# A two-layer convolution and attention kernel: first products fed from the weight sums in SBUF, a first image normalised by two engines, and earlier transposes

## The chip, the cores and the metric

The kernel runs on one NeuronCore of one Trainium2 chip. The metric is the device time of one execution in microseconds (us). Three runs of the kernel before took 2762.28, 2762.81 and 2766.79 us; the median is 2762.81 us. A separate execution was recorded by the hardware profiler; every duration, wait and instant below is from that one.

In the text, PE is the tensor engine (matmul), DVE the vector engine, ACT the scalar engine, POOL the GpSimd engine and SP the engine whose queue issues nearly all DMAs.

## What is computed

Eight images of 768 channels and 32x32 pixels (1024 tokens) pass through two residual layers. Cut to what matters:

```python
# layer 0: attention on a group-normalised image
qkv = gn(x) as tokens @ W_qkv.T            # only k and v are used
scores = var(v) @ var(k).T * scale         # one variance per token and head: rank one
out = softmax(scores) @ v                  # 12 heads of 64
x = x + (out @ W_proj.T + b_proj)
# layer 1: local correlations and a 1x1 convolution
f = gn(x)
corr = 28 shifted products of f / |f| with itself, summed over channels
x = x + (conv_w @ concat(f, corr) + conv_b)
```

All data and weights are float32.

## The kernel before

**The products.** Every large product (keys and values, the projection, the convolution) is split into 2x2 blocks, and the 8 block products are replaced by 7 products of sums of blocks (the scheme of Strassen and Winograd). A product has a number p; the numbers in use order are `ORDER = (1, 5, 6, 3, 7, 4, 2)`. Products 1, 3 and 2 of keys and values take blocks of the weights as they are; 5, 6, 7 and 4 take sums of weight blocks. One unit of `KeysValues.unit` is one such product for one pair of token tiles g: six matmul records of 128x384, because each of three contraction chunks takes two passes. A half (384 columns of the weights) has two rounds d of 14 units in the order of `PAIR`, which alternates two token pairs. The operands on the image's side also need sums, `s`, which POOL makes in `make_sums`: first the sum of two blocks for both pairs (L546), then three more sums from it (L548, L550, L552).

**The weight sums.** `WeightSums(which, ...)` loads four blocks of weights into one buffer (`ws`), and its four steps make the sums on DVE and store each into DRAM (`kvs` for the two halves of keys and values, `tsp` and `tsc` for projection and convolution). `KvStream` then streams the weight blocks of all units through five buffers (`KVBLOCKS`), from the weights themselves or from `kvs`. The buffer of `ws` is the single buffer of the pool `fpool`, which also holds the images `f` and `raw1`; so the sums of the second half can be loaded only when those of the first are done with.

**The first image.** The prologue loads image 0 (`xn`, six chunks of 128x1024) and the weights of sum 0 over the queues of SP and ACT. `first_norm` takes its statistics on DVE, spreads them over groups with two small matmuls, raises to the power -1/2 on POOL (`rstd`), and `Norm.apply` normalises the six chunks on DVE. Between the third and the fourth chunk the first weight sum is made; the other three follow the sixth chunk. All four are stored by DMAs on ACT's queue and loaded back by `KvStream`.

**The order.** Nothing is scheduled by hand on the chip: while the program is written out, an object `Clock` keeps a model time, and work is appended to the engines' queues when its model time has come (`later.after(us, job)`; `later.after_dve(us, job)` counts from the end of the vector work that the model knows). Each engine then runs its queue strictly in order and waits where a semaphore asks for it. So the figures in these calls decide only the order of instructions on each queue.

**One image in steady state** takes about 338 us. Its second half of keys and values, its attention (six pairs of heads; `av` matmuls in bursts of 16 or 32 records), the correlations and the convolution of the image before, its own projection, and the first half of the next image follow each other on PE. `KeysValues.spread` closes each half: DVE computes the variances (`vm`, `km`) and their maximum, POOL spreads the maximum, and then the function `values` transposes the variances of v on PE (`ptv`, L501), DVE copies them (`rsv`), a DMA writes them to DRAM (`vdr`) and DMAs broadcast them to all partitions (`bc`), from which ACT makes exponentials (`ex`, L674), which are what the `av` matmuls stream. `keys` does the same for k (`nk`, `ptk`, `rsk`, `kdr`, `bk`), from which ACT sums denominators (`junk`, L684). For each of the first three pairs of heads, the sums are inverted (`inv`), transposed on PE (`it`), copied (`ir`), written (`di`), broadcast (`rd`), and multiplied into the output (`v<-v,rd` on DVE). There are six buffers of `ex` and two of each of the matmul banks x and y; z products use the y banks.

Of the kernel before, what the change touches and what calls it, by code (L numbers as in the profile page):

```python
# [6 lines left out]
F32 = mybir.dt.float32  # L7
AF = mybir.ActivationFunctionType
ALU = mybir.AluOpType
# [4 lines left out]
P = 128  # L14
NB, C, H, W = 8, 768, 32, 32
# [23 lines left out]
JH = J // 2  # L39
# [23 lines left out]
ORDER = (1, 5, 6, 3, 7, 4, 2)  # L63
# [88 lines left out]
def two_layers(ctx, tc, x, wkv, wproj, bproj, wconv, wcorr, bconv, out):  # L152
    nc = tc.nc

    def pool(name, bufs, **kw):
        return ctx.enter_context(tc.tile_pool(name=name, bufs=bufs, **kw))
# [17 lines left out]
    st = pool("st", 1)  # L174
# [8 lines left out]
    later = clock  # L183
    vector = Vector(nc.vector, clock)
    ready = set()
# [14 lines left out]
    def image_tile(pl, tag, name):  # L200
        return pl.tile([P, J, N], F32, tag=tag, name=name)
# [24 lines left out]
    class WeightSums:  # L226


        def __init__(self, which, *queues):
            self.which = which  # L230
            flat = image_tile(fpool, "f", f"ws{which}").rearrange("p j n -> p (j n)")
            self.at = [flat[:, n * JH * KW : (n + 1) * JH * KW] for n in range(5)]
            for n in range(4):
                r, c = divmod(n, 2)
                queue = queues[n % len(queues)]
                if which in (0, 1):
                    queue.dma_start(out=self.at[n].rearrange("p (k m) -> p k m", k=JH), in_=kv_block(which, r, c))
                else:
                    to = self.at[n].rearrange("p (k m) -> p k m", k=JH)
                    queue.dma_start(out=to, in_=t_block(which, r, c).rearrange("p k i m -> p k (i m)"))  # L240
# [14 lines left out]

        def step(self, engine, p, to, a, b, op, queue):
            engine.tensor_tensor(to, a, b, op)
            self.store(p, to, queue)

        def store(self, p, at, queue):  # L260
# [5 lines left out]

    class KvStream:
        def __init__(self):
            self.keys = [(b, h, d, p) for b in range(NB) for h in range(2) for d in range(2) for p in ORDER]
            self.loaded, self.tiles, self.gone = 0, {}, set()  # L270

        def fill(self, most=None):
# [9 lines left out]

        def done(self, key):
            del self.tiles[key]

            def free():
                self.gone.add(key)
                self.fill()

            later.after(KV_US + 0.3, free)  # L290
# [64 lines left out]
    xn = load(image_tile(xnpool, "xn", "xn0"), xv[0], nc.sync, nc.scalar)  # L355
    sums0 = WeightSums(0, nc.sync, nc.scalar)
    kv_stream, t_stream = KvStream(), TStream()
# [68 lines left out]
    class Norm:  # L426
# [24 lines left out]
            self.rstd = st.tile([P, 1], F32, tag="rstd", bufs=2, name=f"rstd{name}")  # L451
            nc.gpsimd.tensor_tensor(self.rstd, ve, neghalf[:, 0:1], ALU.pow)  # L452

        def apply(self, to, src, key, apart, between=lambda: None):


            def chunk(j):
                vector.tensor_scalar(to[:, j, :], src[:, j, :], self.mean, self.rstd, ALU.subtract, ALU.mult)
                if j + 1 == JH:
                    between()  # L460
                if j + 1 < J:
                    later.after(apart, lambda: chunk(j + 1))
                else:
                    ready.add(key)

            chunk(0)

    def first_norm(b, xn, apart, then):

        bn = gn_tile(f"bn1_{b}")  # L470

        def stats(j):
            for hf in range(2):
                gn_stats(bn, xn, j, hf)
            if j + 1 < J:
                later.after(2 * apart, lambda: stats(j + 1))
            else:
                norm = Norm(bn, f"a{b}")
                later.after_dve(0.3, norm.means)
                later.after_dve(3.0, norm.spreads)  # L480
                later.after_dve(5.0, lambda: then(norm))

        stats(0)
# [22 lines left out]
    class KeysValues:  # L506
# [101 lines left out]
        def spread(self, half):  # L608
            b = self.b
            name = f"{b}_{half}"  # L610
            km2 = st.tile([P, HH, MT], F32, tag="km2", bufs=2, name=f"km2{name}")
            head_m2(self.bn["k", half], km2, f"k{name}")
            top = st.tile([P, HH], F32, tag="top", name=f"top{name}")
            vector.tensor_reduce(top, km2, AX.X, ALU.max)
            most = st.tile([P, HH], F32, tag="most", name=f"most{name}")
            nc.gpsimd.partition_all_reduce(most, top, P, bass_isa.ReduceOp.max)
            m2 = st.tile([P, HH, MT], F32, tag="vm2", bufs=4, name=f"vm2{name}")
            head_m2(self.bn["v", half], m2, f"v{name}")
            nk = st.tile([P, HH, MT], F32, tag="nk", bufs=4, name=f"nk{name}")
            kdr, vdr = [dpool.tile([HH, N], F32, tag=f"{kind}dr", name=f"{kind}dr{name}") for kind in "kv"]  # L620
            for of, new in ((self.m2, m2), (self.nk, nk), (self.kdr, kdr), (self.vdr, vdr)):
                of.append(new)

            def values():
                to_rows(m2, vdr, f"v{name}")
                ready.add(("v", b, half))

            def keys():
                for h in range(HH):
                    vector.tensor_scalar(  # L630
                        nk[:, h, :], km2[:, h, :], most[:, h : h + 1], HD ** -0.5 / (HD - 1) ** 2,
                        ALU.subtract, ALU.mult,
                    )
                ready.add(("nk", b, half))
                if not set(SUMMED[b > 0]).issuperset(range(3 * half, 3 * half + 3)):
                    later.after_dve(0.5, rows)

            def rows():
                to_rows(nk, kdr, f"k{name}")
                ready.add(("k", b, half))  # L640

            later.after_dve(2.5, values)
            later.after_dve(3.5, keys)


    class Pair:
# [538 lines left out]
    def project(b, ots):  # L1185
        f = first_f[0] if b == 0 else image_tile(fpool, "f", f"f{b}")
        for n, us in ((0, 0.0), (1, 0.5), (3, 1.5), (4, 3.0), (2, 12.0), (5, 14.0)) if b else ():
            later.after(us, lambda n=n: nc.sync.dma_start(out=f[:, n, :], in_=xv[b, :, n, :]))
        bn = gn_tile(f"bn2_{b}")
        if b + 1 < NB:  # L1190
            x1_dram[b] = dpool.tile([P, J, N], F32, tag="x1", name=f"x1d{b}")
        left = {(i, hf) for i in range(J) for hf in range(2)}

        def finished(i, hf):
            gn_stats(bn, f, i, hf)
            left.remove((i, hf))
            if b + 1 < NB and (i, 1 - hf) not in left:
                nc.sync.dma_start(out=x1_dram[b][:, i, :], in_=f[:, i, :])
            if not left:
                later.after(0.1, normalise)  # L1200

        def normalise():
            norm = Norm(bn, f"b{b}")
            later.after_dve(0.3, norm.means)
            later.after_dve(3.0, norm.spreads)

            def apply():
                to = f if b + 1 < NB else image_tile(xnpool, "xn", "f_last")
                layer1.append((to, f))
                norm.apply(to, f, ("f", b), 2.0 if b + 1 < NB else 0.0)  # L1210

            later.after_dve(5.0, apply)

        sums = TokenSums(f"o{b}", ots[:JH], ots[JH:])
        clock.wait(("ot", b, JH - 1), ready=ready)
        sums.first()
        wide = Wide("p", f"p{b}", f, bproj_sb, sums.operand, finished)
        late = True
        for n, (us, _, unit) in enumerate(wide.units()):
            if n == 4:  # L1220
                clock.wait(("ot", b, HP - 1), ready=ready)
            if late and n > 1 and ("ot", b, HP - 1) in ready:
                late = False
                sums.second()
                later.after(3.0, sums.thirds)
                later.after(8.0, sums.fourth)
            unit()
            clock.pass_time(us)
# [6 lines left out]
        xn = images[b]  # L1235
        clock.after(12.0, lambda: first_norm(b, xn, 1.2, lambda norm: norm.apply(xn, xn, ("xn", b), 1.2)))

    steps0 = sums0.steps(vector, nc.scalar)
    kv_stream.fill(1)

    def first_sum():
        steps0[0]()
        kv_stream.fill(2)

    first_norm(0, xn, 0.0, lambda norm: norm.apply(xn, xn, ("xn", 0), 0.0, first_sum))
    clock.wait(("xn", 0), ready=ready)
    for step in steps0[1:]:
        step()
    kv_stream.fill()
    images, layer1 = [xn], []  # L1250
    first_f = []

    def sum_weights(which, wait):
        for n, step in enumerate(WeightSums(which, nc.sync).steps(vector, nc.sync)):
            later.after(wait + 3.0 * n, step)

    def load_first_f():
        first_f.append(load(image_tile(fpool, "f", "f0"), xv[0]))
# [17 lines left out]
            later.after(1.0 * n, t_stream.fill)  # L1276

    second = []
    sum_weights(1, 24.0)
    later.after(50.0, lambda: sum_weights("p", 14.0))  # L1280
    later.after(82.0, load_second)
    kv, kv1 = KeysValues(0, xn), KeysValues(1, None)
    work_off(kv.units(0))
    for b in range(NB + 1):
# [6 lines left out]
        if b:  # L1291
# [3 lines left out]
            f, acc = layer1[b - 1] if b > 1 else first_f * 2  # L1295
# [66 lines left out]
```

## Time and profile before

| what | value |
|---|---|
| median of 3 runs | 2762.81 us |
| time of the profiled execution | 2773.49 us |
| its span (first to last instruction) | 2771.8 us |
| granted TensorE clock, mean | 0.993 |
| PE busy | 2712.3 us (98%) |
| DVE busy | 1664.1 us (60%) |
| ACT busy | 1362.3 us (49%) |
| POOL busy | 307.0 us (11%) |
| DMA moved | 451.85 MB, 163 GB/s over the span |

The profiled execution took 10.7 us more than the median of the runs. PE is the engine that is nearly always busy, so the time can be read as PE's work plus the moments in which PE waits or runs slowly. These are few: before 40 us, in the first attention, and a few microseconds in each later image. An idle moment of any other engine matters only where PE then waits for it.

In the answers of the trace, a row of a timeline gives the start in us, the duration in us, the engine, the line, the operation, output<-inputs, the shape and the number of instructions merged into the row; brackets at its end give the engine's idle time just before and what ended it. Ends of matmuls are modelled, so a row of matmuls reads some 0.2 us longer than the distance to the next.

### The profile page before, as it was taken

To read this page: it belongs to the slowest core of one execution; us is meant where nothing else is said; L and a number is where in the kernel's file an instruction comes from. 1 tells how busy PE (TensorE), PEld (TensorE's weight loads), DVE (VectorE), ACT (ScalarE), POOL (GpSimd) and SP (SyncE) were. 2 spreads that over 40 slices of the span, in tenths; PEclk is the share of its full clock that TensorE was granted. 3 is DMA by queue.
4 is the path that set the end of the run, shared out by engine and by line. 5 is a ranking of instruction groups with operands and counts; after the bars stand their busy time and mean duration, and the time that the engine had idled before them with its cause. 6 is when DMAs were issued, how large, how long until landed. Compare 5 with 4: busy or idle time off the path is not lost.

```text
span 2771.8 us, 28821 instructions
## 1 busy us (share of the span) xinstructions
PE 2712.3 (98%) x9063; PEld 1277.7 (46%) x9063; DVE 1664.1 (60%) x4163; ACT 1362.3 (49%) x1814; POOL 307.0 (11%) x350
## 2 busy tenths in 40 slices
PE   6999999999999999999999999999999999999999
PEld 3543454335643455434554346533465334653353
DVE  4858734685447854478534884358743587446853
ACT  1398078520596106970079701886019850298400
POOL 3420101002200031000310012100121001110000
PEclk9999999999999999999999999999999999999999
DMA  8764454545554545536456365563654536535323
GB/s 302 280 227 150 142 189 122 163 165 160 175 150 143 187 154 157 165 128 204 150 158 189 97 203 168 149 181 91 228 175 130 182 97 222 171 113 170 117 73 95
DMA packets 324579, 451.85 MB, mean 163 GB/s; under 512 B 59794, under 2 KB 245890, under 8 KB 324426
## 3 DMA queue, kind: packets, MB, share of 16 engines
q1 hardware_dynamic: 322618, 444.88, 50.8%
q10 hardware_dynamic: 1808, 5.11, 0.5%
q8 instruction: 73, 1.20, 0.2%
q14 instruction: 80, 0.66, 0.1%
HBM read 380.44 MB, written 67.38 MB: 162 GB/s over the span
## 4 chain that ended last, share of the span: by engine, by line
PE 74%; issue 10%; DMA 5%; ACT 5%; DVE 4%; SPq 1%; POOL 1%; DVEq 0%; POOLq 0%; ACTq 0%
PE x L342 29%; PE av L699 17%; PE y L342 14%; PE z L342 8%; ACT ex L674 3%; PE gr L1006 2%; DMA rd<-di 2%; ACT junk L684 2%; DMA bc<-vdr 1%; DVE dn L146 1%; PE den L732 1%; PE z L936 1%; PE x L936 1%; PE den L782 1%; DVE cs L146 0%
## 5 line engine op out<-in xcount | busy, mean ns | idle before, releaser
L674 ACT ACTIVATE ex<-bc,nk 128x1024 f32<-128x1024 f32 x768 | 834.5, 1138 | 493.6 <-DMA bc<-vdr 271.3
L699 PE MATMUL av<-ex,v 128*64 128x512 f32 x3072 | 709.1, 601 | 12.3 <-ACT ex L674 12.3
L684 ACT ACTIVATE junk<-bk,vm 128x1024 bf16<-128x1024 f32 x368 | 420.5, 1143 | 41.9 <-DMA bk<-kdr 35.6
L699 PEld LDWEIGHTS av<-ex,v 128*64 128x64 f32 x3072 | 218.7, 138 | 473.9 <-issue 394.4
L146 DVE TENSOR_TENSOR acc<-acc,ex 128x1024 f32<-128x1024 f32 x350 | 401.6, 1212 | 0.0
L209 ACT COPY kp<-x 128x384 f32<-128x384 f32 x28 | 13.3, 479 | 558.1 <-PE x L342 558.1
L342 PE MATMUL y<-kv,s 128*128 128x384 f32 x768 | 267.8, 489 | 2.6 <-DMA kv<-kvs 2.6
L342 PE MATMUL x<-kv,xn 128*128 128x384 f32 x768 | 263.9, 490 | 4.4 <-DVE xn L146 3.3
L342 PE MATMUL x<-kv,s 128*128 128x384 f32 x768 | 262.2, 489 | 3.3 <-POOL s L546 3.3
L342 PEld LDWEIGHTS x<-kv,xn 128*128 128x128 f32 x768 | 145.1, 191 | 108.6 <-issue 14.3
L342 PEld LDWEIGHTS x<-kv,s 128*128 128x128 f32 x768 | 145.4, 191 | 104.1 <-issue 6.8
L342 PEld LDWEIGHTS y<-kv,s 128*128 128x128 f32 x768 | 142.4, 190 | 102.1 <-issue 8.7
L1006 PE MATMUL gr<-f 128*128 128x227 f32 (+1 forms) x672 | 131.8, 346 | 0.0
L342 PE MATMUL z<-kv,xn 128*128 128x384 f32 x384 | 130.1, 488 | 0.0
L342 PE MATMUL x<-v,wt 128*128 128x512 f32 x288 | 130.0, 596 | 0.0
L1006 PEld LDWEIGHTS gr<-f 128*128 128x128 f32 x672 | 121.2, 190 | 18.7 <-issue 6.2
L146 DVE TENSOR_TENSOR v<-y,v 128x128 f32<-128x128 f32 x180 | 40.9, 282 | 136.5 <-PE y L342 136.5
L342 PE MATMUL x<-f,wt 128*128 128x512 f32 x252 | 115.4, 598 | 0.1
L452 POOL TENSOR_TENSOR rstda<-vea,neghalf 128x1 f32<-128x1 f32 x8 | 4.8, 597 | 930.2 <-DVE vea L146 930.2
L546 POOL TENSOR_TENSOR s<-xn 128x384 f32<-128x384 f32 x64 | 68.5, 1080 | 309.6 <-PE x L342 219.4
L146 DVE BATCH_NORM_STATS2 vbn<-v 128x6 f32<-128x64 f32 x720 | 101.7, 210 | 0.0
L146 DVE COPY acc<-ex 128x1024 f32<-128x1024 f32 x50 | 33.7, 703 | 107.6 <-ACT junk L684 36.8
(170 smaller groups left out, 2925.0 us busy)
## 6 DMA issues: line engine op xcount, KB each, us to landing
kv<-kvs SPq DMA_DIRECT2D x128, 576.0 KB
kv<-in_wkv_dram SPq DMA_DIRECT2D x96, 576.0 KB
bc<-vdr SPq DMA_DIRECT2D x96, 512.0 KB
f<-in_x_dram SPq DMA_DIRECT2D x48, 512.0 KB
bk<-kdr SPq DMA_DIRECT2D x46, 512.0 KB
x1d<-f SPq DMA_DIRECT2D x42, 512.0 KB
x<-x1d SPq DMA_DIRECT2D x42, 512.0 KB
out_dram<-x SPq DMA_DIRECT2D x84, 256.0 KB
```

The lines of the kernel that those rows point to most:

```text
L146: return getattr(self.engine, name)(*args, **kw)
L209: nc.scalar.copy(to, at)
L342: nc.tensor.matmul(t, lhsT=lhsT, rhs=rhs, start=p in FIRST and k == 0, stop=stop and k == len(pairs) - 1, skip_group_check=True,)
L452: nc.gpsimd.tensor_tensor(self.rstd, ve, neghalf[:, 0:1], ALU.pow)
L546: nc.gpsimd.tensor_tensor(self.sums[g][:, 0], a[g][2], a[g][3], ALU.add)
L674: nc.scalar.activation(ex, self.bc[e], AF.Exp, scale=self.kv.nk[self.half][:, h, t : t + 1])
L684: nc.scalar.activation(junk, self.bk[e], AF.Exp, scale=self.kv.m2[self.half][:, h, t : t + 1], accum_out=self.sums[:, e, t : t + 1],)
L699: nc.tensor.matmul(self.av[e * HD : (e + 1) * HD, hf, :], lhsT=self.vt[:, t, e, :], rhs=exs[e][:, hf * HF : (hf + 1) * HF], start=t == 0, ...
L732: nc.tensor.matmul(den[at * 32 : (at + 1) * 32, :], lhsT=ones[:, 0:32], rhs=self.acc[e][:, hf * HF : (hf + 1) * HF], start=True, stop=True,)
L782: nc.tensor.matmul(den[e * HD : (e + 1) * HD, :], lhsT=ones, rhs=self.acc[e][:, at], start=True, stop=True)
L936: nc.tensor.matmul(t, lhsT=wcorr_sb[at, i, :], rhs=cs[at, tokens, :], start=False, stop=True, skip_group_check=True)
L1006: nc.tensor.matmul(ps[:, :n], lhsT=f[:, j, t * P : (t + 1) * P], rhs=f[:, j, t * P : t * P + n], start=j == 0, stop=j == J - 1,)
```

## The change

1. In `WeightSums.step`, for the first half's sums alone, each sum in SBUF is entered into `kv_stream.tiles` under the key of image 0, half 0, round 0, and so is the block `at[3]` for product 3. The units of that round for p = 5, 6, 7, 4 and 3 then read the buffer of `ws`. The stream's list of keys leaves these five out, and `done` doesn't free a stream buffer for them. The sums are still stored to DRAM for later rounds, now by SP's queue and no longer by ACT's.
2. For image 0, `Norm.apply_both` takes the place of `Norm.apply`: DVE computes a shift, -mean x rstd, and normalises chunks 0 to 2; ACT normalises chunks 3 to 5 by an activation with scale and bias. All four weight sums follow on DVE.
3. The weight sums of the second half are planned later and closer together (a start at 26 on the model clock, steps 9 us after it and 1.5 us apart, where they stood at 24 and 3 us apart).
4. From image 1 on, the transposes of `values` and `keys` are planned 1.0 and 2.2 us after the vector work before them, where they stood at 2.5 and 3.5.
5. For image 0, the chunks of `f` are normalised 1.0 us apart on the model clock, where they stood 2.0 apart.

```diff
--- before.py
+++ after.py
@@ -255,6 +255,9 @@
 
         def step(self, engine, p, to, a, b, op, queue):
             engine.tensor_tensor(to, a, b, op)
+            if self.which == 0:
+                for q, at in ((p, to), (3, self.at[3])):
+                    kv_stream.tiles[0, 0, 0, q] = at.rearrange("p (k m) -> p k m", k=JH)
             self.store(p, to, queue)
 
         def store(self, p, at, queue):
@@ -266,7 +269,11 @@
 
     class KvStream:
         def __init__(self):
-            self.keys = [(b, h, d, p) for b in range(NB) for h in range(2) for d in range(2) for p in ORDER]
+
+            self.keys = [
+                (b, h, d, p)
+                for b in range(NB) for h in range(2) for d in range(2) for p in ORDER if p in (1, 2) or b + h + d
+            ]
             self.loaded, self.tiles, self.gone = 0, {}, set()
 
         def fill(self, most=None):
@@ -282,6 +289,8 @@
 
         def done(self, key):
             del self.tiles[key]
+            if key not in self.keys:
+                return
 
             def free():
                 self.gone.add(key)
@@ -451,13 +460,20 @@
             self.rstd = st.tile([P, 1], F32, tag="rstd", bufs=2, name=f"rstd{name}")
             nc.gpsimd.tensor_tensor(self.rstd, ve, neghalf[:, 0:1], ALU.pow)
 
-        def apply(self, to, src, key, apart, between=lambda: None):
+        def apply_both(self, t, key):
+
+            shift = st.tile([P, 1], F32, tag="shift", name=f"shift{self.name}")
+            vector.scalar_tensor_tensor(shift, self.mean, -1.0, self.rstd, ALU.mult, ALU.mult)
+            for j in range(JH):
+                vector.tensor_scalar(t[:, j, :], t[:, j, :], self.mean, self.rstd, ALU.subtract, ALU.mult)
+                nc.scalar.activation(t[:, JH + j, :], t[:, JH + j, :], AF.Identity, bias=shift, scale=self.rstd)
+            ready.add(key)
+
+        def apply(self, to, src, key, apart):
 
 
             def chunk(j):
                 vector.tensor_scalar(to[:, j, :], src[:, j, :], self.mean, self.rstd, ALU.subtract, ALU.mult)
-                if j + 1 == JH:
-                    between()
                 if j + 1 < J:
                     later.after(apart, lambda: chunk(j + 1))
                 else:
@@ -639,8 +655,8 @@
                 to_rows(nk, kdr, f"k{name}")
                 ready.add(("k", b, half))
 
-            later.after_dve(2.5, values)
-            later.after_dve(3.5, keys)
+            later.after_dve(1.0 if b else 2.5, values)
+            later.after_dve(2.2 if b else 3.5, keys)
 
 
     class Pair:
@@ -1207,7 +1223,7 @@
             def apply():
                 to = f if b + 1 < NB else image_tile(xnpool, "xn", "f_last")
                 layer1.append((to, f))
-                norm.apply(to, f, ("f", b), 2.0 if b + 1 < NB else 0.0)
+                norm.apply(to, f, ("f", b), (2.0 if b else 1.0) if b + 1 < NB else 0.0)
 
             later.after_dve(5.0, apply)
 
@@ -1235,24 +1251,20 @@
         xn = images[b]
         clock.after(12.0, lambda: first_norm(b, xn, 1.2, lambda norm: norm.apply(xn, xn, ("xn", b), 1.2)))
 
-    steps0 = sums0.steps(vector, nc.scalar)
-    kv_stream.fill(1)
-
-    def first_sum():
-        steps0[0]()
-        kv_stream.fill(2)
-
-    first_norm(0, xn, 0.0, lambda norm: norm.apply(xn, xn, ("xn", 0), 0.0, first_sum))
+    steps0 = sums0.steps(vector, nc.sync)
+    kv_stream.fill(2)
+
+    first_norm(0, xn, 0.0, lambda norm: norm.apply_both(xn, ("xn", 0)))
     clock.wait(("xn", 0), ready=ready)
-    for step in steps0[1:]:
+    for step in steps0:
         step()
     kv_stream.fill()
     images, layer1 = [xn], []
     first_f = []
 
-    def sum_weights(which, wait):
+    def sum_weights(which, wait, apart=3.0):
         for n, step in enumerate(WeightSums(which, nc.sync).steps(vector, nc.sync)):
-            later.after(wait + 3.0 * n, step)
+            later.after(wait + apart * n, step)
 
     def load_first_f():
         first_f.append(load(image_tile(fpool, "f", "f0"), xv[0]))
@@ -1276,7 +1288,7 @@
             later.after(1.0 * n, t_stream.fill)
 
     second = []
-    sum_weights(1, 24.0)
+    later.after(26.0, lambda: sum_weights(1, 9.0, 1.5))
     later.after(50.0, lambda: sum_weights("p", 14.0))
     later.after(82.0, load_second)
     kv, kv1 = KeysValues(0, xn), KeysValues(1, None)
```

## The prediction

> **What bounds the kernel now.** I read the page first, for the share of each engine: PE is busy for 98% of the span. So only moments in which PE waits or runs slowly can be won, and the second view is the list of waits, PE's alone (waited for: us in total, times, longest).
>
> ```profile
> PE pma L437 <- DVE mva L146: 13.9, 1, 13.9
> PE av L699 <- ACT ex L674: 12.3, 15, 5.0
> ...
> PE x L342 <- POOL s L546: 3.3, 1, 3.3
> PE x L342 <- DVE xn L146: 3.3, 1, 3.3
> PE y L342 <- DMA kv<-kvs: 2.6, 1, 2.6
> ```
>
> PE's idle time is 2771.8 - 2712.3 = 59.5 us. The first is the load and the statistics of image 0, which the change leaves alone. The last three stand before 40 us; the second is spread over the images. The third view is the timeline of the start.
>
> ```profile
> 22.36 3.89 DVE L146 TENSOR_TENSOR ws<-ws 128x1152 f32<-128x1152 f32 x3
> ...
> 22.52 5.53 POOL L546 TENSOR_TENSOR s<-xn 128x384 f32<-128x384 f32 x2 [5.81 <-DVE xn L146]
> ...
> 27.43 4.11 PE L342 MATMUL y<-kv,s 128*128 128x384 f32 x12 [2.63 <-DMA kv<-kvs]
> ...
> 34.87 5.80 PE L342 MATMUL x<-kv,s 128*128 128x384 f32 x12 [3.33 <-POOL s L546]
> ```
>
> PE's second pair of units waits 2.63 us for a weight sum that goes to DRAM and back, and for POOL's first sum, whose two instructions take 5.53 us instead of 2.0. The next pair waits 3.33 us. POOL had made the second sum by 29.98, so what came last was the reload of the next weight sum, whatever the row names. That pair then takes 5.80 us for twelve records that take 3.87 later. The fourth view is the timeline of image 3 at the end of its second half.
>
> ```profile
> 1149.49 0.27 PE L808 MATMUL it<-ident,inv 128*16 128x128 f32 x1
> ...
> 1161.42 0.29 PE L501 MATMUL ptv<-ident,vm 128*48 128x128 f32 x1 [0.35 <-DVE vm L146]
> ...
> 1170.53 1.23 DVE L146 TENSOR_TENSOR v<-v,rd 128x1024 f32<-128x1024 f32 x1 [3.68 <-DMA rd<-di]
> ...
> 1180.18 6.58 ACT L674 ACTIVATE ex<-bc,nk 128x1024 f32<-128x1024 f32 x6 [7.45 <-DMA bc<-vdr]
> ...
> 1182.66 9.30 PE L699 MATMUL av<-ex,v 128*64 128x512 f32 x30 [0.21 <-ACT ex L674]
> ```
>
> DVE's copy of the transposed variances (`rsv`, 1171.67) stands in its queue behind the multiplication that waits for `rd`; so `vdr`, `bc` and the exponentials are late, and PE loses 1.55 + 0.3 us idle and 2.3 us in a burst that takes 9.30 where 30 records take 6.6.
>
> **What the Trainium skill says.** "SBUF — State Buffer", section "Who interferes with whom": a DVE instruction with two SBUF inputs and a GpSimd instruction that reads SBUF exclude each other; the second blocks until the first ends. The trace agrees: POOL's first sum takes 4576 ns against 991 to 998 for the others, and ends 0.85 us after DVE's three. "TensorE: Matmul & The Clock Gate", "Part 1: The HAM clock gate": after an idle window of some 3.4 us, free-running, the array runs at half speed until it has been busy that long. Here the first six records after idle times of 3.30 and 3.33 us came every 0.64 us and later ones every 0.32; after 2.63 us all were fast.
>
> **Start-up, step by step** (instants of the profiled execution).
> - `rstd` ends at 16.71. The new shift is a small DVE instruction like `ea` (0.22 us); three chunks (2.26 for three) end at 19.2, where they ended at 19.0. ACT starts at 17.0. No row shows this activation; the nearest, `ex` with one per-row operand, takes 1138 ns, so three end at 20.5. Bounds 20.2 to 21.2; nothing hangs on it, as POOL is blocked longer. Its table load (1.28 us), late in the trace behind the stores on ACT's queue, falls before 13 us.
> - PE's first two units start at 19.2 and, cold, take 5.7: to 24.9 (before 24.8).
> - DVE makes the four weight sums from 19.2, 1.30 us each: to 24.4. Their loads are done by then: DMA is near idle from 18 us.
> - POOL may start at 20.5 but is locked out until 24.4; its first sum ends at 25.3, the second at 26.3, and the next two at 27.3 and 28.2. The lock takes back most of ACT's help.
> - PE: second pair 25.3 to 29.2, third 29.2 to 33.1. No sum goes through DRAM, the idle gap shrinks to 0.4 us, and the array stays warm. The unit at 40.51 starts at 33.1: **7.4 us earlier**. Bounds: 5.5, if the third pair goes cold again (1.9); 8.3, if DVE's sums leave POOL gaps.
>
> Costed at nothing: five stream loads less (2.9 MB) cover 7.4 us less time to load in. Product 2's early load (576 KB) stands behind product 1's and is needed near 45. The stores on SP hold it until the last sum at 24.4; behind them is round 1's first block, needed at 48. Loads of the second half's sums now wait until PE has read `ws`, about 45; 2.36 MB at some 280 GB/s land near 54, and the four sums (5.3 us) end near 57. DVE's next work behind them is wanted at 62, and the stream block behind those loads on SP at 62 too, landing near 56. Without that cover of some 5 us each microsecond late would be one lost.
>
> **Transposes, step by step** (images 2 to 7; the instructions' order comes from building both versions).
> - In half 0, `keys` pulls `ptk` one unit forward, and the stream of `bk` stands before a `kv` load that waited for its buffer (1057.39; `bk` 1058.13, landing 1065.1). Every `av` burst of the first three pairs stands one unit, 1.94 us, earlier. ACT's first exponentials end by 1060.7, before the burst's new place at 1061.5; the fourth step's must end 5.3 us later. In the trace it had 0.3 us to spare; with `bk` 3 to 4 us earlier I take no wait. Bound: 1.6 us per image.
> - In half 1 `it` moves one unit forward, `ir` no longer stands behind the vector products of `cs`, and `rd` has one load of 512 KB and one of 192 KB less before it: 0.7 MB at the 264 GB/s of that stretch are 2.7 us. Multiplication, `rsv`, `bc` and exponentials follow 2.4 us earlier (bounds 0 and 3.1, `it` plus `ir`).
> - `ptv` now stands before a convolution unit of 2.58 us and after 24 instead of 16 records of `av` (0.22 us each): 0.8 to 0.9 us sooner, while `vm` hangs on a load of x (1157.17) that hardly moves. PE's wait there grows from 0.1 to 0.45 us to 0.7 to 1.0, and the rest of the burst and all units queue behind it.
> - DVE takes the first y product after `rd` and the next sums; the third y product needs its bank. `rd` + 4.85 us against 1173.06 in image 3: hidden if `rd` gains over 2.2 us there, 1.0 in image 2, 0.9 and 0.5 in 4 and 5.
>
> Loss per image before (idle and stretch of `ptv` and the first burst), less the gain of 2.4, but not under the new `ptv` wait: image 2: 3.3 to 0.9; 3: 4.95 to 2.55; 4: 3.0 to 1.0; 5: 3.1 to 1.0; 6: 1.5 to 0.8; 7: 1.35 to 1.0. That is 9.95. Image 1 waits 5.04 us at 511.50 behind `rd`; its `bc` loads, ahead of it, start 2.4 us earlier: 2.4. Sum 12.35; as landings differ between images by some 2 us, I take **10**. Bounds 0 and 15.
>
> The closer `f` chunks of image 0: the last waited 2.05 us for a store that lands at 370.74 and will wait about 6; behind it stand 3.1 us of vector work, done near 374.6, and PE wants their banks at 377.46. Nothing, bounds -0.5 and +2.
>
> **Sum.** 7.4 + 10 = 17.4 us off 2773.49, the time of the execution whose durations I used. It stands 10.7 us above the median of the runs; the steps are the same in both, so I take them off the median: 2762.8 - 17.4 = **2745.4**.
>
> **Rivals.**
> - *Only the start pays*: `rd` lands no earlier (its tail in the trace is slow: 15 to 22 GB/s after 1169), and the transposes win what the earlier `ptv` costs. 2762.8 - 7.4 = 2755.4. For it: landings hang on all traffic. Against: 0.7 MB less stands in front.
> - *Only the transposes pay*: the gain of the start is lost in image 0's attention, where from 139 to 180 us the chain of waits runs through ACT. 2752.8. Against: ACT's work there begins with PE's, and moves with it.
> - *Slower*: bursts pulled forward by a unit find their exponentials late, because neither `bk` nor `rd` lands earlier. Per image 1.6 (fourth step) + 0.7 (`ptv`) + 0.8 (third y bank: 1.0, 2.3, 0.9, 0.5 and twice nothing, averaged) = 3.1; times six 18.6; 2762.8 - 7.4 + 18.6 = 2774. It decides from 1.2 us per image, where it eats the start's gain, and is measurably slower from 2.2. For it: DMA runs at 0.5 of its time and in clumps. Against: both loads stand earlier in SP's queue.
> - That the change doesn't do what it says: the built order shows the five products reading `ws`, so I give this no share of its own.
>
> **Numbers.** A measurement of this kernel can tell 0.2%, 5.5 us, from no change. Chances: forecast 0.62, start alone 0.17, transposes alone 0.09, slower 0.12. Faster by more: 0.60 + 0.12 + 0.07 = 0.79; same 0.10; slower 0.11. The range 2738 to 2759 takes in start 5.5 to 8.3 with transposes 0 to 15, and leaves out the slower rival and the tails.
>
> **What would show it.** Right: no PE wait for `kvs` before 40 us; twelve records of the third pair in about 4 us; the fourth pair near 33; `ptv` waits near 5 us in all; PE's waits for `ex` at half of 12.3 or less; in image 3 the multiplication by `rd` still some 20.6 us after `it`, but 2.4 us earlier against PE's units, and the burst of 9.30 near 7. Wrong: a new PE wait on DVE before y products, or on ACT in the first burst of images 2 to 7; a wait for `kv` or `ws` between 45 and 65 us.

## The result, and the profile after

| | before | after |
|---|---|---|
| median of 6 runs each | 2764.61 us | 2748.69 us |
| lowest and highest | 2762.28, 2766.79 | 2747.49, 2750.54 |
| profiled execution, time and span | 2773.49, 2771.8 us | 2747.85, 2746.1 us |

The ratio of the times is 0.9943, with a 95% interval of 0.9931 to 0.9955: 15.9 us faster, 0.57%. The forecast was 17.4 us off the median, 2745.4; it lay 3.3 us under the result. The two profiled executions differ by 25.6 us, because that of before ran 9 us above its median; so differences of instants late in the two traces overstate the gain, and below only stretches within a trace are compared.

The list of waits of the changed kernel, PE's alone (waited for: us in total, times, longest):

```profile
PE pma L446 <- DVE mva L146: 13.9, 1, 13.9
PE ptv L517 <- DVE vm L146: 9.4, 6, 2.3
PE av L715 <- ACT ex L690: 6.8, 4, 4.6
```

No wait for `kvs` and none for `s` is left. The waits for `ex` went from 12.3 to 6.8 us, and all four that are left lie in images 0 and 1; a new row, `ptv` behind `vm`, has 9.4 us in six waits, one in each of the images 2 to 7.

The timeline of the start (instant, duration, engine, line, operation, output<-inputs, shape, number; in brackets the idle time before and what ended it):

```profile
16.76 2.25 DVE L146 TENSOR_SCALAR xn<-xn,meana,rstda 128x1024 f32<-128x1024 f32 x3
16.88 3.50 ACT L469 ACTIVATE xn<-xn,shifta,rstda 128x1024 f32<-128x1024 f32 x3 [6.79 <-DVE shifta L146]
18.93 6.88 DVE L146 TENSOR_TENSOR ws<-ws 128x1152 f32<-128x1152 f32 x4
19.03 6.11 PE L351 MATMUL x<-kv,xn 128*128 128x384 f32 x12 [3.31 <-DVE xn L146]
20.46 4.13 POOL L562 TENSOR_TENSOR s<-xn 128x384 f32<-128x384 f32 x2 [3.81 <-ACT xn L469]
...
24.98 4.03 PE L351 MATMUL y<-ws,s 128*128 128x384 f32 x12
...
28.85 4.03 PE L351 MATMUL x<-ws,s 128*128 128x384 f32 x12
...
32.72 2.10 PE L351 MATMUL y<-ws,s 128*128 128x384 f32 x6
```

From 19.03 us on PE's rows join without a bracket. The first pair, behind an idle time, takes 6.11 us for its twelve records (the array is called cold below), both pairs behind it take 4.03 (warm). The unit that began at 40.51 begins at 32.72: 7.8 us earlier.

The timeline of image 3 at the end of its second half:

```profile
1133.27 0.27 PE L824 MATMUL it<-ident,inv 128*16 128x128 f32 x1
...
1140.56 5.37 PE L715 MATMUL av<-ex,v 128*64 128x512 f32 x24
...
1142.71 0.75 DVE L146 SCALAR_TENSOR_TENSOR x<-x,bconv_sb,x 128x512 f32<-128x512 f32 x1 [4.30 <-DMA x<-x1d]
...
1146.97 0.29 PE L517 MATMUL ptv<-ident,vm 128*48 128x128 f32 x1 [1.04 <-DVE vm L146]
...
1152.61 1.22 DVE L146 TENSOR_TENSOR v<-v,rd 128x1024 f32<-128x1024 f32 x1
...
1159.97 1.15 ACT L690 ACTIVATE ex<-bc,nk 128x1024 f32<-128x1024 f32 x1 [3.46 <-DMA bc<-vdr]
...
1165.77 7.09 PE L715 MATMUL av<-ex,v 128*64 128x512 f32 x32
```

The exponentials now begin 5.8 us before the burst that reads them, and its 32 records take 7.09 us, what they take anywhere unhindered; before, the burst was split, waited 1.55 us and took 9.30 for 30 records. DVE no longer idles for `rd` there. What is new is the 1.04 us in front of `ptv`.

To compare kernels below, one number is used beside the times: **the loss of images 2 to 7**, the sum over PE's timeline from 600 to 2640 us of two things: idle times over 0.15 us, and for each row the part beyond 0.35 us of what it takes longer than its number of records times their undisturbed pitch (0.22 us for a record of `av`). It was 19.0 us before and is 11.6 after. It is read from one execution each and moves by about 1 us with the pitch chosen, so it is a guide to where the time goes, and the times decide. That of before is from the execution that ran 9 us above its median; the start alone, with the same transposes, has 16.2.

### The profile page after: what moved, and what is told of

It is laid out like the page before. It is cut to its first block, busy times and chain, and to the rows that moved or that the text cites. A ratio compares the mean times of both kernels' runs of the same rounds, so it can differ in the third digit from the quotient of the medians.

```text
span 2746.1 us, 28839 instructions
## 1 busy us (share of the span) xinstructions
PE 2692.0 (98%) x9063; PEld 1273.1 (46%) x9063; DVE 1663.3 (61%) x4161; ACT 1358.8 (49%) x1817; POOL 306.0 (11%) x350
## 4 chain that ended last, share of the span: by engine, by line
PE 83%; issue 8%; DVE 4%; DMA 3%; ACT 2%; POOL 0%; SPq 0%; DVEq 0%; POOLq 0%; ACTq 0%
PE x L351 32%; PE av L715 20%; PE y L351 16%; PE z L351 9%; PE gr L1022 3%; DMA x<-x1d 1%; DVE dn L146 1%; ACT ex L690 1%; ACT junk L700 1%; PE den L748 1%; PE z L952 1%; PE x L952 1%; PE den L798 1%; PE y L952 1%; DVE cs L146 1%
## 5 line engine op out<-in xcount | busy, mean ns | idle before, releaser
L715 PE MATMUL av<-ex,v 128*64 128x512 f32 x3072 | 696.0, 600 | 6.8 <-ACT ex L690 6.8
L351 PE MATMUL y<-kv,s 128*128 128x384 f32 x744 | 258.8, 488 | 0.0
L351 PE MATMUL x<-kv,s 128*128 128x384 f32 x744 | 254.6, 488 | 0.0
L351 PEld LDWEIGHTS x<-kv,xn 128*128 128x128 f32 x756 | 142.0, 191 | 116.9 <-issue 19.5
L351 PEld LDWEIGHTS x<-kv,s 128*128 128x128 f32 x744 | 139.1, 190 | 102.9 <-issue 14.9
L351 PE MATMUL x<-f,wt 128*128 128x512 f32 x252 | 115.3, 598 | 0.0
L351 PEld LDWEIGHTS z<-kv,xn 128*128 128x128 f32 x384 | 72.3, 190 | 49.9 <-issue 3.0
```

What stands on the lines that cost most here:

```text
L351: nc.tensor.matmul(t, lhsT=lhsT, rhs=rhs, start=p in FIRST and k == 0, stop=stop and k == len(pairs) - 1, skip_group_check=True,)
L715: nc.tensor.matmul(self.av[e * HD : (e + 1) * HD, hf, :], lhsT=self.vt[:, t, e, :], rhs=exs[e][:, hf * HF : (hf + 1) * HF], start=t == 0, ...
```

## The experiments

The theory: start and transposes are two separate gains that add up; of the transposes, half 0's bring the whole gain, and half 1's own earlier place is cost. The rivals stand in the expectations. All times are medians, with the ratio to the kernel before, measured on the same chip, and its 95% interval.

| kernel | median us | ratio to before | loss of images 2 to 7 |
|---|---|---|---|
| changed kernel | 2748.7 | 0.9943 (0.9931 to 0.9955) | 11.6 |
| start only | 2756.0 | 0.9978 (0.9966 to 0.9989) | 16.2 |
| transposes only | 2756.9 | 0.9975 (0.9968 to 0.9983) | 11.6 |
| half 0 early | 2740.0 | 0.9918 (0.9904 to 0.9932) | 2.8 |
| half 1 early | 2759.5 | 0.9985 (0.9978 to 0.9992) | 21.9 |
| keys of half 0 early | 2738.9 | 0.9909 (0.9894 to 0.9924) | 5.6 |
| no ACT in the normalisation | 2748.8 | 0.9952 (0.9936 to 0.9968) | 12.7 |
| old plan of the second sums | 2751.5 | 0.9957 (0.9942 to 0.9973) | 13.0 |

**Start only.**

```diff
-            later.after_dve(1.0 if b else 2.5, values)
-            later.after_dve(2.2 if b else 3.5, keys)
+            later.after_dve(2.5, values)
+            later.after_dve(3.5, keys)
...
-                norm.apply(to, f, ("f", b), (2.0 if b else 1.0) if b + 1 < NB else 0.0)
+                norm.apply(to, f, ("f", b), 2.0 if b + 1 < NB else 0.0)
```

> The changed kernel with the transposes back at 2.5 and 3.5 and the chunks of f at 2.0 for every image: only the start-up is changed. Start and transposes add up (A): the unit that began at 40.51 us begins near 32.7, nothing later gives it back, and the median is 7 to 8.5 us under that of the kernel before. The start's gain is lost in the first attention (B): 0 to 2 us under it. The start does nearly all (C): 13 to 16 us under it.

Measured: 6.1 us under the kernel before by the ratio (3.0 to 9.4); the unit begins at 32.70, and the medians differ by 7.6. That is A, and B and C are out. The loss of images 2 to 7 isn't above that of before, so the start's gain is not given back there. From 297 to 412 us, where the chunks of `f` of image 0 are made, PE's rows stand 115.3 us apart in this kernel, with the old distance of the chunks, and 115.6 in the changed one: that part of the change moves nothing.

**Transposes only.**

```diff
-            later.after_dve(2.5, values)
-            later.after_dve(3.5, keys)
+            later.after_dve(1.0 if b else 2.5, values)
+            later.after_dve(2.2 if b else 3.5, keys)
```

> The kernel before with the transposes at 1.0 and 2.2 from image 1 on, the start-up left alone. A (the two parts add up): 7.5 to 9 us under the kernel before, with six waits of PE for vm before ptv of 1.0 to 2.3 us (9 us in all) and waits of PE for ex of 7 us or less. B (the transposes do all): 14 us or more under it. C (they do nothing): within 2 us of it.

Measured: 6.9 us under it (4.7 to 8.8), six `ptv` waits of 8.2 us in all, and waits for `ex` of 7.7. A comes nearest, though the gain is a little under its 7.5 to 9 us and the waits for `ex` a little over its 7; B and C are out. The two parts sum to 13.0 us of the 15.8 that the ratio gives for both, within their intervals. Taken the other way, as the changed kernel less the start alone, the transposes are worth 9.7 us, so their value is known only as some 7 to 10.

**Half 0 early, half 1 late.**

```diff
-            later.after_dve(1.0 if b else 2.5, values)
-            later.after_dve(2.2 if b else 3.5, keys)
+            later.after_dve(2.5 if half or not b else 1.0, values)
+            later.after_dve(3.5 if half or not b else 2.2, keys)
```

> The changed kernel, but in half 1 the transposes stand at 2.5 and 3.5 again; half 0's stay at 1.0 and 2.2. By the built order the bursts of av and it keep their earlier places, and ptv of half 1 goes behind all 32 records of the burst (1.75 us later on PE than behind 24). A (the gain comes from half 0, and half 1's earlier ptv is pure cost): the six ptv waits, 9.4 us in the changed kernel, fall to under 2, the exponentials come 0.5 to 1 us later without making PE wait, and the median is 6 to 9 us under the changed kernel's (2740 to 2743). B (the earlier ptv is what brings the exponentials in time): the wait moves to PE's first burst behind them, and the median is at the changed kernel's or up to 5 us over it.

The timeline of image 3 in this kernel:

```profile
1136.40 0.27 PE L824 MATMUL it<-ident,inv 128*16 128x128 f32 x1
...
1143.69 7.09 PE L715 MATMUL av<-ex,v 128*64 128x512 f32 x32
...
1145.80 0.75 DVE L146 SCALAR_TENSOR_TENSOR x<-x,bconv_sb,x 128x512 f32<-128x512 f32 x1 [4.25 <-DMA x<-x1d]
...
1150.71 0.29 PE L517 MATMUL ptv<-ident,vm 128*48 128x128 f32 x1
...
1163.59 12.79 ACT L690 ACTIVATE ex<-bc,nk 128x1024 f32<-128x1024 f32 x12 [2.67 <-DMA bc<-vdr]
...
1167.65 7.09 PE L715 MATMUL av<-ex,v 128*64 128x512 f32 x32
```

PE finishes all 32 records and only then comes to `ptv`, whose `vm` (done at 1150.02) is ready: no bracket. The exponentials still begin 4.1 us before their burst. Measured 2740.0 us; all `ptv` waits together fell from 9.4 to 0.2 us. That is A: 22.7 us under the kernel before by the ratio, against 15.8 for the changed kernel. The intervals of these two just touch, but the `ptv` rows, and a loss that falls by 8.8, show where the difference of 6.9 us comes from.

**Half 1 early, half 0 late.** The same two lines with `half and b` in place of `b`.

> The changed kernel, but in half 0 the transposes stand at 2.5 and 3.5; only half 1's are early. By the built order the bursts of av and it are at their old places, and ptv stands behind 20 records of the burst instead of 24. A (the gain comes from half 0): the ptv waits grow by 0.5 to 0.9 us each, the waits for ex stay near 12 us, and the median is that of the start alone plus 3 to 5 us, 2759 to 2762. B (half 1's earlier ptv brings the gain): at the changed kernel's median, 2747 to 2750.

PE's timeline in image 3:

```profile
1146.71 1.94 PE L715 MATMUL av<-ex,v 128*64 128x512 f32 x8
1150.77 0.29 PE L517 MATMUL ptv<-ident,vm 128*48 128x128 f32 x1 [2.12 <-DVE vm L146]
1150.99 7.07 PE L715 MATMUL av<-ex,v 128*64 128x512 f32 x24
```

`ptv` stands in the middle of the burst, waits 2.12 us, and the 24 records behind it take 7.07 us, where 24 take 5.37 in the changed kernel. PE's row has no wait for ACT there: the weight loads of the same stretch show the array at half speed (last section). The waits sum to 12.2 us and the loss is the largest of all, 21.9. The median is 4.1 us under the kernel before (2.2 to 6.1), in the range of A. Against the start alone, half 1's part costs 2.0 us by the ratios and 5.7 by the loss. The intervals of the two ratios overlap, so the times alone don't show a cost; the rows do. A's sentence that the waits for `ex` stay near 12 us was wrong: they are 7.3, and none of them stands in images 2 to 7, because PE, held up at `ptv`, comes later to the bursts. The lateness is paid at another place.

**Keys of half 0 alone.** Of the four settings only one is kept early.

```diff
-            later.after_dve(1.0 if b else 2.5, values)
-            later.after_dve(2.2 if b else 3.5, keys)
+            later.after_dve(2.5, values)
+            later.after_dve(3.5 if half or not b else 2.2, keys)
```

> The changed kernel, with one of its four settings for images 1 to 7 left: keys of half 0 at 2.2; values of both halves and keys of half 1 stand at 2.5 and 3.5 again. By the built order the bursts of av and the first its keep the earlier places of the changed kernel, ptv of half 1 stands behind all 32 records of its burst, and the it after it one unit later than where half 0 has both settings. A (keys of half 0 bring the whole gain): 8 to 10 us under the changed kernel (2738 to 2742), with losses of PE in images 2 to 7 under 4 us. B (values of half 0 matter too): at the changed kernel's median or above it, with waits for ex back in the second halves.

Measured 2738.9 us, 25.2 us under the kernel before (21.0 to 29.3), and its interval lies wholly below that of the changed kernel. The loss is 5.6 us, just above the 4 of A. So one setting of four brings the whole gain of the transposes. This kernel and the one with both settings of half 0 are the fastest of all, and the runs can't tell these two apart. PE's rows in half 0 of image 3 show why, first of the kernel before, then of this one:

```profile
1046.93 0.27 PE L501 MATMUL ptv<-ident,vm 128*48 128x128 f32 x1
1047.04 4.04 PE L342 MATMUL y<-kv,s 128*128 128x384 f32 x12
1050.91 0.27 PE L501 MATMUL ptk<-ident,nk 128*48 128x128 f32 x1
```

```profile
1034.52 0.27 PE L517 MATMUL ptv<-ident,vm 128*48 128x128 f32 x1
1034.63 2.10 PE L351 MATMUL y<-kv,s 128*128 128x384 f32 x6
1036.57 0.27 PE L517 MATMUL ptk<-ident,nk 128*48 128x128 f32 x1
```

`ptk` has moved forward by one unit of six records, while `ptv` stands where it stood. It stands there too with both settings of half 0 early: its setting for `values` moves nothing on PE.

**No ACT in the normalisation.**

```diff
-    first_norm(0, xn, 0.0, lambda norm: norm.apply_both(xn, ("xn", 0)))
+    first_norm(0, xn, 0.0, lambda norm: norm.apply(xn, xn, ("xn", 0), 0.0))
```

> The changed kernel, but VectorE normalises all six chunks of image 0 and then makes the four weight sums. The chunks end near 21.2 us instead of 20.4, and POOL's first sum and VectorE's weight sums are released by the same engine. A (POOL and VectorE take turns, as in the changed kernel): POOL's first pair takes about 4.1 us and ends near 25.6, and the unit that stands at 32.72 us stands at 33.3 to 34, so the half that ScalarE took over is worth 0.6 to 1.3 us. B (POOL is held until VectorE's last weight sum, as the prediction had it): POOL's first sum takes 5 us or more and ends near 27.4, its second near 28.4, the unit stands at 35 to 37, and ScalarE's half is worth 2.5 to 4.5 us.

Its timeline of the start:

```profile
16.76 4.42 DVE L146 TENSOR_SCALAR xn<-xn,meana,rstda 128x1024 f32<-128x1024 f32 x6 [0.77 <-POOL rstda L461]
19.20 6.16 PE L351 MATMUL x<-kv,xn 128*128 128x384 f32 x12 [3.40 <-DMA kv<-in_wkv_dram]
21.11 7.56 DVE L146 TENSOR_TENSOR ws<-ws 128x1152 f32<-128x1152 f32 x4
21.27 4.11 POOL L562 TENSOR_TENSOR s<-xn 128x384 f32<-128x384 f32 x2 [4.54 <-DVE xn L146]
25.20 4.03 PE L351 MATMUL y<-ws,s 128*128 128x384 f32 x12
...
32.94 2.10 PE L351 MATMUL y<-ws,s 128*128 128x384 f32 x6
```

POOL takes 4.11 us for its pair although VectorE released it, so A has the mechanism, and B is out. But the unit stands at 32.94, 0.2 us later than in the changed kernel and earlier than either expected: VectorE ends its chunks only 0.8 us after ScalarE would have, and the pair's first operand is ready before PE is done with its first, cold units at 25.2. ScalarE's half is worth nothing that can be measured. What is left of the start's gain then belongs to feeding PE from `ws`, with the weight sums in one row and their stores on SP; these were not run apart.

**Old plan of the second half's sums.**

```diff
-    later.after(26.0, lambda: sum_weights(1, 9.0, 1.5))
+    sum_weights(1, 24.0)
```

> The changed kernel, but the weight sums of the second half keep their plan of before (24 on the model clock, 3 us apart). Their loads then stand one stream block earlier in SP's queue, and wait there for PE's last use of the first sums, near 45 us. A (the move is covered on both sides): no wait of PE between 40 and 80 us, and the median is within 2 us of the changed kernel's. B (the move was needed): a wait of PE of 2 to 6 us for a stream block or behind VectorE between 48 and 66 us, and the median is higher by that.

Its timeline, VectorE and PE:

```profile
51.53 1.36 DVE L146 TENSOR_TENSOR ws<-ws 128x1152 f32<-128x1152 f32 x1 [6.48 <-DMA ws<-in_wkv_dram]
52.80 0.55 DVE L146 TENSOR_TENSOR kp<-z,kp 128x384 f32<-128x384 f32 x1
...
53.45 2.17 PE L351 MATMUL y<-kv,s 128*128 128x384 f32 x6 [1.59 <-issue]
...
56.37 2.17 PE L351 MATMUL y<-kv,s 128*128 128x384 f32 x6 [0.74 <-DVE kp L146]
```

The first sum stands in VectorE's queue ahead of the addition that empties the bank of `z` (one of the y banks), and waits 6.48 us for its load; so PE waits for the bank twice. The row names "issue" for the first wait, but it ends 0.1 us after that addition. The median is 2.8 us above the changed kernel's; the ratios differ by 0.0014, within their intervals. B, shown by the trace; the median alone would not prove it. So the new plan avoids a loss that the first part would bring; whether it would gain anything without the first part was not run.

## Why the prediction came out as it did

**Start-up, 7.4 us: right, measured 7.8** in the trace and 3.0 to 9.4 in the runs. The term that was mis-sized is POOL's lock. The prediction took from before that POOL stands still until DVE's last sum (24.4), and put its first two sums at 25.3 and 26.3. They ended at 22.5 and 24.6, because the two engines took turns. This is the case behind the upper bound that it named, "if DVE's sums leave POOL gaps", and it came true at DVE's expense: the four sums took 6.88 us, not 5.2. So there was no gap of 0.4 us at 24.9; what sets the second pair's start is the first pair's end, cold until 24.98. The Trainium skill's "TensorE: Matmul & The Clock Gate", "Part 1: The HAM clock gate", which the prediction used for the pace after long idle windows, is borne out for that pace: the first pair, after 3.31 us of idling, took 6.11 us for twelve records, the two behind it 4.03 each.

"The lock takes back most of ACT's help" had the right outcome for the wrong reason: the help is nil because PE's first pair is still running.

**Loads of the second half's sums, nothing: right, with less to spare.** The loads were issued at 44.52, DVE waited for them twice (1.83 and 1.70 us), and the sums ended at 58.64 rather than near 57. The cover of 5 us was 3.4. The old plan shows what stood behind it: PE's banks. DVE's two waits are, to the letter, a sign of being wrong that the prediction named, a wait for `ws` between 45 and 65 us; PE has no wait there.

**Transposes, 10 us: right in sign, measured 6.9** (4.7 to 8.8) without the start and 9.7 beside it. Its terms:

- *Half 0's bursts one unit earlier, at no cost*: right. No wait of PE for `ex` stands in images 2 to 7, here or in the two kernels with half 0 alone early.
- *Exponentials of half 1 earlier by 2.4 us*: more than that, and from partly another source. Worked out from the timelines of images 2 to 6, the time between the first exponential and the place of the burst that reads it was 0.9 us before and is 4.3 with half 0 alone early (7.0 in the changed kernel, where PE's waits at `ptv` delay the burst). Of these 3.4 us, 1.2 come from `it`, which begins 30.1 instead of 28.9 us ahead of the `cs` products that stand before the burst; this is the unit that it moved, less the waits and small items in between, and the prediction had it. The multiplication by `rd` followed `it` after 19.6 us before, 18.5 with the start alone and 19.5 with half 0 early: the 0.7 MB less in front of `rd` brought no measurable haste, and that step failed. In its place came one that the prediction had not looked at: from `rsv` to the first exponential it took 8.2 us before and 8.3 with the start alone, and 6.1 with half 0 early (5.9 in the changed kernel), the other 2.1. In image 3, SP's queue had a load of x between `vdr` and `bc`, at 1172.36 before, which now stands ahead of `vdr`. With half 1 alone early that load is out of the way too, and yet the time is 8.8 us, so its place is not the whole cause. In image 3 of that kernel `bc` was issued 3.5 us after `vdr`, against 2.0 in the changed kernel, with `rd` still on its way; whether that is the reason stays open.
- *`ptv` waits of 0.7 to 1.0 us per image, 5 us in all*: the step that failed most, 9.4 us. In images 2 and 3 they were 0.97 and 1.04, as forecast; in 4 and 6 they were 2.34 and 2.12, in 5 and 7 1.40 and 1.50. The prediction held that the load of x on which `vm` hangs "hardly moves". In image 4 DVE waited 4.62 us for it before and 5.61 after, so it landed a microsecond later against DVE's other work. There the array was also cold behind the longer wait: the 8 records took 3.59 us instead of 1.94, which the forecast had no term for. The rows are below.
- *Image 1, 2.4 us*: not there. Its wait went from 5.04 to 4.61 us and the 8 records behind it from 4.71 to 3.93; with half 0 early the wait is 6.03 us, with the start alone 5.74. Its `bc` loads gain nothing reliably.
- *The third y bank*: no loss in the changed kernel. It exists: with keys of half 0 alone PE waited 0.74 us there in image 3, until 4.7 us after the start of the multiplication by `rd`, near the 4.85 of the forecast.
- *The burst of 9.30 in image 3*: its 30 records took 2.7 us over 6.6, not the 2.3 that the prediction read.

Image 4, DVE's wait for the load of x before, then the same and PE's rows in the changed kernel:

```profile
1496.80 0.75 DVE L146 SCALAR_TENSOR_TENSOR x<-x,bconv_sb,x 128x512 f32<-128x512 f32 x1 [4.62 <-DMA x<-x1d]
```

```profile
1479.37 0.75 DVE L146 SCALAR_TENSOR_TENSOR x<-x,bconv_sb,x 128x512 f32<-128x512 f32 x1 [5.61 <-DMA x<-x1d]
...
1483.62 0.29 PE L517 MATMUL ptv<-ident,vm 128*48 128x128 f32 x1 [2.34 <-DVE vm L146]
1483.84 3.59 PE L715 MATMUL av<-ex,v 128*64 128x512 f32 x8
```

That the sum came near is partly luck, because errors of opposite sign cancelled in part: the lateness of the exponentials went away wholly in images 2 to 7, and not down to 2 or 3 us in image 3, while `ptv` cost 4.4 us more and image 1 gained nothing that can be told. The loss fell from 19.0 to 11.6 us, and 9.4 of these 11.6 are the waits at `ptv`. Two of the signs that the prediction named say the same: `ptv` waits near 5 us were 9.4, and waits for `ex` at half of 12.3 or less were 6.8.

**The rivals.** Both parts pay, so "start alone" (2755.4) and "transposes alone" (2752.8) describe the two single kernels, not this one. The slower rival failed: it needed bursts that are pulled forward and find their exponentials late, and in the five kernels where the bursts of half 0 stand earlier beside the new start no wait for `ex` is left in images 2 to 7; with the transposes alone, one of 0.36 us is. Its term for `ptv`, 0.7 us per image, was too small: 1.6 on average.

**The working's own choice**, to take the gain off the median and not off the profiled execution, was right: the execution profiled before was the outlier, 6.7 us above the slowest of the six runs in the table.

## What to carry to other kernels

When a set of work is moved earlier, try its members one at a time: here one of four moves brought all of the gain, and the two of half 1 together took back 7 us by putting an instruction with a late operand into the middle of a burst on the busiest engine. An instruction whose operand hangs on a load should stand behind work that PE can do anyway. And before a second engine is brought in to help, look at what the consumer is doing when the help would arrive.

## What the hardware showed unexpectedly

PE's weight loads in image 3 of the kernel with half 1 early, around the wait at `ptv`:

```profile
1150.77 0.10 PEld L517 LDWEIGHTS ptv<-ident,vm 128*48 128x48 f32 x1 [3.00 <-DVE vm L146]
...
1152.93 0.25 PEld L715 LDWEIGHTS av<-ex,v 128*64 128x64 f32 x2 [0.61 <-ACT junk L700]
1153.79 0.24 PEld L715 LDWEIGHTS av<-ex,v 128*64 128x64 f32 x2 [0.61 <-issue]
1154.64 0.24 PEld L715 LDWEIGHTS av<-ex,v 128*64 128x64 f32 x2 [0.61 <-issue]
1155.31 0.14 PEld L715 LDWEIGHTS av<-ex,v 128*64 128x64 f32 x2 [0.43 <-issue]
1155.74 0.14 PEld L715 LDWEIGHTS av<-ex,v 128*64 128x64 f32 x2 [0.29 <-issue]
```

Two loads come every 0.85 us until about 1155 and every 0.43 from then on: half speed for some 3 us behind a gap of 3.0 us between loads, which costs 1.7 us on top of the wait (7.07 us less 5.37). Five of the six `ptv` waits of that kernel show it; one of 2.15 us doesn't, and of the changed kernel's only that of 2.34 us does. That it comes and goes fits the statement of the Trainium skill's "TensorE: Matmul & The Clock Gate", "Part 1: The HAM clock gate", that the window in which activity is counted runs free. The length doesn't fit: the section gives about 3.4 us for the idle window, and here waits of 1.83 to 2.34 us, with 3.0 us between the loads in the rows shown, were enough in six cases; the measurement decides. The same pace, two loads every 0.85 us, stands in image 3 before, in the burst of 9.30 us: part of what the prediction read as late exponentials was a cold array. In this kernel a wait of PE of some 2 us can thus cost nearly twice what it reads.

Rows of single instructions, the changed kernel, DVE and POOL:

```profile
20.32 1.36 DVE L146 TENSOR_TENSOR ws<-ws 128x1152 f32<-128x1152 f32 x1
20.46 2.07 POOL L562 TENSOR_TENSOR s<-xn 128x384 f32<-128x384 f32 x1 [3.81 <-ACT xn L469]
21.59 2.15 DVE L146 TENSOR_TENSOR ws<-ws 128x1152 f32<-128x1152 f32 x1
```

POOL's sum, 1.0 us by itself, takes 2.07: DVE's instruction ends near 21.6, and POOL's some 0.9 us later. Then DVE's next, 1.35 by itself, takes 2.15: it ends some 1.2 us after POOL's sum. They go on in turn: 2.10 and 2.15 for the next two. The Trainium skill's "SBUF — State Buffer", section "Who interferes with whom", has such instructions exclude each other for their whole length, and that "issue order, not op shape, decides who blocks". Both agree. But before the change POOL's first sum waited through three instructions of DVE in a row (4.58 us). It is not the engine that releases POOL: without ACT, DVE releases it, and they still take turns. Nor is it when POOL starts: it started 0.14 to 0.16 us after the start of a sum of DVE in each of these three kernels. What decides whether POOL gets its turn between two DVE instructions was not found.
